# VectorE in written order, wider statistics for image 0 and a rearranged end, in a two-layer attention kernel

## The chip, the cores and the metric

The kernel runs on one core of one Trainium2 chip. The metric is the device time of one execution in microseconds (us), the median of several runs.

## The reference, cut to what matters

Two attentions follow each other on 8 images of 64 channels and 64 x 64 = 4096 positions, all in float32.

```python
# layer 0: 8-channel f and g, 64-channel values
f, g, hh = Wf @ x + bf, Wg @ x + bg, Wh @ x + bh
x = x + hh @ softmax(f^T g, axis=2)^T
# layer 1: group norm (8 groups), then 64-channel attention
xn = (x - mu) * rsqrt(var + 1e-5) * gamma + beta
q, k, v = split(w_qkv @ xn + b_qkv)
out = x + w_proj @ attention(q, k, v, scale=64**-0.5) + b_proj
```

## The kernel before

The work is laid out as a list of *stages*, one per layer and image, in the order L0 image 0, L0 image 1, L1 image 0, L0 image 2, L1 image 1 and so on. A stage has 4 chunks of 512 queries, and a chunk 16 *steps*. In each step TensorE makes scores into PSUM, ScalarE takes their exponentials into one of six `e` buffers, TensorE multiplies the `e` of the step before by the values into accumulators, and VectorE adds that `e` into a running sum, `esum` (128 x 2048 elements, 2.29 us). Everything else (projections, copies of values, statistics of the group norm, reciprocals) is a *unit of work* due at a given step, for a later stage or a former chunk.

```python
def pair():                       # PSUM: 8 banks; three pairs rotate
    if lent is not None: return pairs[lent]
    turn += 1; return pairs[turn % 3]

def values(self, src, w, c):      # values of the next image, chunk c
    ps = pair()
    ...                           # 64x64 matmuls into ps
    first_ = self.kind == self.b == c == 0
    copy = nc.vector.tensor_copy if lent is None or first_ else nc.scalar.copy
    copy(self.vt[:, :, ts(c, TPC), :], ps[...])

def weigh(i, j, e, cols, now):    # values x e, and the add into esum
    at.weigh(acc, e[:, p], t, p, j == 0, j == 2 * NT - 1, cols)
    ...
    with tc.issue_after(layers0[0].split.ins) if i == 0 and t == 1 else nullcontext():
        added = nc.vector.tensor_add(esum, first if t == 1 else esum, e).ins
    if t == NT - 1:
        finished(i, now)          # copies the accumulators away (total), later sums and result

def total(self, raw, acc):        # layer 1: VectorE empties both accumulator banks
    nc.vector.tensor_copy(raw, acc[0])
    return nc.vector.tensor_add(raw, acc[1], raw)

def ended():                      # end of a step: first the due units, then weigh
    for u in due: u[2]()
    for r in batch: weigh(*r, now)
```

Names in the views: `banks` is PSUM; `vt_l` holds values; `v_l` of 128 x 512 holds values of layer 1, but `v_l` of 128 x 1 the variance of the group norm, and `mu_l` its mean; `xn_l` is the normalised input; `raw_l` takes the accumulators; `full_l`, `high_l` and `fg_l` are a projection of layer 0, its cast and the result of splitting it; `kq_l` is what scores are made from.

In this kernel only TensorE is held to the order of the program text. VectorE's instructions are ordered by a scheduler at build time, with a few hints (`issue_after`).

## Time and profile before

| | before |
|---|---|
| median of the first 3 runs | 3088.32 us (3088.18 to 3089.82) |
| span of the profiled run | 3087.7 us |
| TensorE busy | 3050.4 us (99%) |
| VectorE busy | 2534.7 us (82%) |

Two views carry the reading. The first is the page's line of busy tenths, the span in 40 slices of 77 us: each digit is the busy share of a slice in tenths.

```profile
DVE  7998877899768997689876898779987799876676
```

VectorE (DVE) is at nine tenths in the second and third slice, that is up to 231 us. The second is the table by windows; each row is a stretch, its length, then the busy time of PE (TensorE's matmuls), PEld (its weight loads), DVE (VectorE), ACT (ScalarE) and POOL (GpSimd), with the number of instructions, and then the granted clock of TensorE, the share of the DMA engines and GB/s.

```profile
28.00:60.00 32.00, 32.00 (x249) 12.02 (x248) 30.82 (x16) 27.22 (x26) 0.00 (x0) 1.00 0.44 107
141.00:222.00 81.00, 79.25 (x470) 27.43 (x468) 78.61 (x44) 66.23 (x54) 0.00 (x0) 1.00 0.03 8
222.00:262.00 40.00, 30.22 (x148) 10.14 (x148) 35.60 (x34) 21.27 (x21) 0.00 (x0) 0.83 0.03 7
```

From 222 to 262 us, where the statistics of image 0 are made, TensorE works only 30.2 of 40 us and at a clock of 0.83; in the two stretches ahead it has hardly a gap. VectorE has hardly a gap up to 222 us.

### The profile page before, as it was taken

How to read it: one execution, taken by the hardware profiler on the slowest of the kernel's cores; microseconds unless marked ns; L12 is line 12 of the kernel's file. 1: busy time of each engine (PE TensorE's matmuls, PEld its weight loads, DVE VectorE, ACT ScalarE, POOL GpSimd, SP SyncE). 2: the span in 40 equal slices, each digit the busy share in tenths (PEclk: the TensorE clock that was granted, in tenths of full speed). 3: DMA queues.
4: the chain of work that ended last, by engine and by line, in shares of the span. 5: the costliest groups of instructions: out<-in, count | busy, mean ns of one | idle time of the engine just before them, and what ended most of it. 6: DMA issues, size and time to landing. Idle time of an engine off the chain costs nothing.

```text
span 3087.7 us, 59407 instructions
## 1 busy us (share of the span) xinstructions
PE 3050.4 (99%) x26083; PEld 1133.9 (37%) x26083; DVE 2534.7 (82%) x1612; ACT 2043.5 (66%) x1999; POOL 16.5 (1%) x45
## 2 busy tenths in 40 slices
PE   8999999999999999999999999999999999999998
PEld 3333334333343333433334333343333333333433
DVE  7998877899768997689876898779987799876676
ACT  6876655786557865578655785558855588555554
POOL 2000000000000000000000000000000000000000
PEclk9999999999999999999999999999999999999999
DMA  3000010100101001010010100100001000000000
GB/s 78 22 8 11 18 39 15 32 1 15 39 15 32 1 15 39 22 25 1 15 39 22 25 1 17 41 22 22 1 25 36 19 8 1 15 22 15 9 15 12
DMA packets 57531, 62.54 MB, mean 20 GB/s; under 512 B 30816, under 2 KB 30864, under 8 KB 57264
## 3 DMA queue, kind: packets, MB, share of 16 engines
q1 hardware_dynamic: 56192, 58.38, 7.6%
q8 instruction: 206, 3.38, 0.4%
q14 instruction: 61, 0.50, 0.1%
q0 software_dynamic: 672, 0.12, 0.0%
q10 hardware_dynamic: 400, 0.17, 0.0%
HBM read 25.06 MB, written 8.65 MB: 11 GB/s over the span
## 4 chain that ended last, share of the span: by engine, by line
PE 94%; DVE 4%; issue 1%; ACT 1%; DMA 0%; SPq 0%; DVEq 0%; ACTq 0%
PE banks L137 94%; DVE esum_l L749 3%; ACT e_l L836 0%; ACT e_l L877 0%; DVE vt_l L322 0%; DMA x<-in_x_dram 0%; DVE esum_l L386 0%; DVE esum_l L335 0%; ACT full_l L501 0%; SPq L166 0%; DVE high_l L506 0%; DVE diag L401 0%; DVE w_l L589 0%; DVE raw_l L374 0%; DVE x L540 0%
## 5 line engine op out<-in xcount | busy, mean ns | idle before, releaser
L749 DVE TENSOR_TENSOR esum_l<-esum_l,e_l 128x2048 f32<-128x2048 f32 x895 | 2050.1, 2291 | 462.0 <-ACT e_l L836 403.8
L836 ACT ACTIVATE e_l<-banks 128x1024 f32<-128x1024 f32 x1024 | 992.9, 1021 | 800.2 <-PE banks L137 776.8
L137 PE MATMUL banks<-e_l,v_l 64*64 64x512 f32 (+2 forms) x8772 | 1102.7, 589 | 0.0
L877 ACT ACTIVATE e_l<-banks 128x2048 f32<-128x2048 f32 (+3 forms) x765 | 956.2, 1314 | 195.7 <-PE banks L137 188.5
L137 PE MATMUL banks<-kq_l 64*64 64x512 f32 (+1 forms) x8448 | 1009.8, 586 | 2.5 <-ACT mu_l L567 1.2
L137 PE MATMUL banks<-e_l,vt_l 128*64 128x512 f32 (+1 forms) x4060 | 832.1, 550 | 0.0
L137 PEld LDWEIGHTS banks<-e_l,v_l 64*64 64x64 f32 (+1 forms) x8772 | 362.6, 133 | 576.1 <-issue 529.2
L137 PEld LDWEIGHTS banks<-kq_l 64*64 64x64 f32 (+1 forms) x8448 | 348.0, 135 | 577.7 <-issue 545.8
L137 PEld LDWEIGHTS banks<-e_l,vt_l 128*64 128x64 f32 x4060 | 266.9, 136 | 471.5 <-issue 451.4
L137 PE MATMUL banks<-fg_l 32*128 32x512 f32 x1792 | 209.5, 459 | 4.9 <-ACT e_l L877 3.3
L749 DVE TENSOR_TENSOR esum_l<-e_l,e_l 128x2048 f32<-128x2048 f32 x64 | 146.4, 2288 | 11.4 <-ACT e_l L836 9.4
L137 PEld LDWEIGHTS banks<-fg_l 32*128 32x128 f32 x1792 | 85.3, 182 | 187.4 <-ACT e_l L877 138.7
L335 DVE TENSOR_TENSOR esum_l<-esum_l 128x1024 f32<-128x1024 f32 x63 | 76.8, 1219 | 0.7
L654 DVE COPY raw_l<-banks 128x512 f32<-128x512 f32 x31 | 21.4, 691 | 31.3 <-PE banks L137 31.3
L628 ACT ACTIVATE kq_l<-banks,qkb 128x512 f32<-128x512 f32 x64 | 40.6, 696 | 3.8 <-PE banks L137 3.8
L374 DVE TENSOR_TENSOR raw_l<-raw_l,r_l 128x512 f32<-128x512 f32 x63 | 43.1, 684 | 0.0
L137 PE MATMUL banks<-esum_l,ones 128*32 128x256 f32 x504 | 40.3, 391 | 1.6 <-DVE vt_l L322 1.6
L137 PE MATMUL banks<-xn_l,wqk 64*64 64x512 f32 x256 | 34.3, 607 | 4.0 <-DVE xn_l L596 4.0
L137 PEld LDWEIGHTS banks<-wh,x 64*64 64x64 f32 x1024 | 23.2, 138 | 15.6 <-issue 14.4
L137 PEld LDWEIGHTS banks<-wvp,xn_l 64*64 64x64 f32 x1024 | 20.6, 134 | 16.8 <-issue 16.8
L536 ACT COPY raw_l<-banks 128x512 f32<-128x512 f32 x32 | 19.0, 595 | 11.6 <-PE banks L137 11.4
L540 DVE SCALAR_TENSOR_TENSOR x<-raw_l,hb,x 128x512 f32<-128x512 f32 x32 | 24.0, 751 | 1.1
(108 smaller groups left out, 391.7 us busy)
## 6 DMA issues: line engine op xcount, KB each, us to landing
r_l<-recips SPq DMA_DIRECT2D x126, 128.0 KB, 2.9
fg_l<-high_l SPq DMA_DIRECT2D x216, 64.0 KB, 2.0
kq_l<-kq_l SPq DMA_DIRECT2D x64, 128.0 KB, 2.3
out_dram<-raw_l SPq DMA_DIRECT2D x62, 128.0 KB, 2.4
x<-in_x_dram SPq DMA_DIRECT2D x30, 256.0 KB, 4.7
zt_l<-zs_l SPq DMA_DIRECT2D x252, 1.0 KB, 1.7
kq_l<-high_l SPq DMA_DIRECT2D x32, 64.0 KB, 2.0
recips<-stash SPq DMA_DIRECT2D x63, 4.0 KB, 1.4
```

Source lines behind the costliest of these rows:

```text
L137: in_order(nc.tensor.matmul(*args, **kwargs))
L335: nc.vector.tensor_add(esum[:, 0], esum[:, 0], esum[:, 1])
L374: nc.vector.tensor_mul(raw, raw, r)
L536: nc.scalar.copy(raw, acc[0])
L540: nc.vector.scalar_tensor_tensor(xc, o, hb, xc, op0=ALU.add, op1=ALU.add)
L628: nc.scalar.activation(self.parts[:, h, cols], ps[:, h, :], AF.Identity, bias=k1["qkb"][:, h : h + 1],)
L654: nc.vector.tensor_copy(raw, acc[0])
L749: added = nc.vector.tensor_add(esum, first if t == 1 else esum, e).ins
L836: nc.scalar.activation(e[:, p], both_ps[p], AF.Exp, scale=at.scale)
L877: nc.scalar.activation(e.rearrange("k p h n -> k (p h) n")[:, first_ : first_ + n_, :], banks[:, bank : bank + n_, :], AF.Exp, scale=at.scale,
```

## The change

Its intent is to take VectorE's order out of the scheduler's hands. Every VectorE instruction goes through a wrapper that ties it behind the one written before it. The statistics of image 0 are spaced one step wider, and the last chunk's code is put into the order in which its inputs come. The core of the diff:

```diff
+    class InOrder:
+        def __getattr__(self, name):
+            def made(*args, **kwargs):
+                in_order(getattr(nc.vector, name)(*args, **kwargs), "vector")
+            return made
+    vector = InOrder()
 ...                                  # then nc.vector.* -> vector.* everywhere, hints removed, e.g.
-            with tc.issue_after(layers0[0].split.ins) if i == 0 and t == 1 else nullcontext():
-                added = nc.vector.tensor_add(esum, first if t == 1 else esum, e).ins
+            vector.tensor_add(esum, first if t == 1 else esum, e)
 ...                                  # Layer1.before(): statistics, all images and image 0
-            at = [18, 21, 24] if self.b == 0 else [16, 20, 24]
+            at = [18, 22, 26] if self.b == 0 else [16, 20, 24]
-                s = 30 + 8 * c
+                s = 31 + 8 * c if self.b == 0 else 30 + 8 * c
-                    (s - 3, lambda c=c: normal(c), False),
+                    (s - 4, lambda c=c: normal(c), False),
 ...                                  # end(): the accumulators ahead of the reciprocal
+            self.total(raw, acc)
-            nc.vector.reciprocal(rt, z)
-            bounds(rt, 1)
+            vector.reciprocal(rt, z)
 ...                                  # each half's broadcast matmul right behind its diag;
 ...                                  # bounds and n_bad behind both
-            self.residual(raw, c, (nc.sync, nc.scalar))
+            self.residual(raw, c)     # both stores started by one engine
```

More of the change, by code (lines that the diff above doesn't have):

```diff
@@ L1 @@
-from contextlib import ExitStack, nullcontext
+from contextlib import ExitStack
 import concourse.bass as bass
@@ L120, in pair, with in_order @@
         return pairs[turn % 3]
-    tensor_last = None
-    def in_order(made):
-        nonlocal tensor_last
-        if tensor_last is not None:
+    made_last = {}
+    def in_order(made, engine="tensor"):
+        if engine in made_last:
             tc.add_manual_dep(
                 made.ins,
-                tensor_last.name,
+                made_last[engine].name,
                 mybir.DependencyInfo(mybir.DependencyClass.NoSync, mybir.DependencyReason.DATA),
@@ L133, in in_order @@
             )
-        tensor_last = made.ins
+        made_last[engine] = made.ins
+    class InOrder:
[4 more added lines that the diff above has]
+    vector = InOrder()
     def matmul(*args, **kwargs):
@@ L320, in values @@
             first_ = self.kind == self.b == c == 0
-            copy = nc.vector.tensor_copy if lent is None or first_ else nc.scalar.copy
+            copy = vector.tensor_copy if lent is None or first_ else nc.scalar.copy
             copy(
@@ L330, in finish @@
             raw = work.tile([P, CW], F32, tag="raw", bufs=4, name=f"raw_{n}")
-            copied = self.total(raw, acc)
+            self.total(raw, acc)
             zt = small.tile([P, QP], F32, tag="zt", bufs=4, name=f"zt_{n}")
             width = CW // 2
-            with tc.issue_after(copied.ins if self.kind == 1 else added):
-                nc.vector.tensor_add(esum[:, 0], esum[:, 0], esum[:, 1])
+            vector.tensor_add(esum[:, 0], esum[:, 0], esum[:, 1])
             r = None
@@ L364, in reciprocals @@
                 rt = stash[:, ts(index, QP)]
-                nc.vector.reciprocal(rt, zt)
+                vector.reciprocal(rt, zt)
                 broadcast()
@@ L373, in result @@
             def result():
-                nc.vector.tensor_mul(raw, raw, r)
+                vector.tensor_mul(raw, raw, r)
                 self.residual(raw, c)
@@ L383, in end @@
             total = esum[:, 0]
-            with tc.issue_after(added):
-                for part in (esum[:, 1], e[:, 0], e[:, 1]):
-                    nc.vector.tensor_add(total, total, part)
+            for part in (esum[:, 1], e[:, 0], e[:, 1]):
+                vector.tensor_add(total, total, part)
             z, laid = pair()[:, 0, 0:QP], pair()[:, 0, :]
@@ L394, in end @@
                 )
+            raw = work.tile([P, CW], F32, tag="raw", bufs=4, name="raw_end")
+            self.total(raw, acc)
             rt = small.tile([P, QP], F32, tag="zt", bufs=4, name="rt")
-            nc.vector.reciprocal(rt, z)
-            bounds(rt, 1)
-            raw = work.tile([P, CW], F32, tag="raw", bufs=4, name="raw_end")
+            vector.reciprocal(rt, z)
             diag = work.tile([P, QP, P], F32, tag="full", bufs=1, name="diag")
             for h in range(2):
-                nc.vector.tensor_mul(
+                vector.tensor_mul(
                     diag[:, ts(h, TPC), :],
@@ L405, in end @@
                 )
-            self.total(raw, acc)
-            for i in range(2):
-                matmul(bad_ps, bad[:, i : i + 1], ones[:, 0:1], start=i == 0, stop=i == 1)
-            nc.vector.tensor_copy(n_bad, bad_ps)
-            for h in range(2):
                 matmul(
@@ L414, in end @@
                 )
-            nc.vector.tensor_mul(raw, raw, laid)
-            self.residual(raw, c, (nc.sync, nc.scalar))
+            bounds(rt, 1)
+            for i in range(2):
+                matmul(bad_ps, bad[:, i : i + 1], ones[:, 0:1], start=i == 0, stop=i == 1)
+            vector.tensor_copy(n_bad, bad_ps)
+            vector.tensor_mul(raw, raw, laid)
+            self.residual(raw, c)
     class Layer0(Attention):
@@ L481, in project_direct @@
                 )
-                nc.vector.tensor_copy(high[:, i, :], full[:, i, :])
-                nc.vector.scalar_tensor_tensor(
+                vector.tensor_copy(high[:, i, :], full[:, i, :])
+                vector.scalar_tensor_tensor(
                     dst[:, 0:CW], high[:, i, :].bitcast(F32), lowmask2[:, i : i + 1],
@@ L502, in project @@
             high = work.tile([P, 2, CW], F32R, tag="high", bufs=1, name=f"high_{n}")
-            nc.vector.tensor_copy(high[rows], full[rows])
+            vector.tensor_copy(high[rows], full[rows])
             split = high
-            self.split = nc.vector.scalar_tensor_tensor(
+            vector.scalar_tensor_tensor(
                 split[rows], high[rows].bitcast(F32), lowmask[rows, :], full[rows],
@@ L539, in residual @@
             xc = x_tiles[self.b][:, ts(c, CW)]
-            nc.vector.scalar_tensor_tensor(xc, o, hb, xc, op0=ALU.add, op1=ALU.add)
-            nc.vector.bn_stats(self.st[:, c, :], xc)
+            vector.scalar_tensor_tensor(xc, o, hb, xc, op0=ALU.add, op1=ALU.add)
+            vector.bn_stats(self.st[:, c, :], xc)
     class Layer1(Attention):
@@ L560, in channels @@
             def channels():
-                nc.vector.bn_aggr(mv, self.st())
+                vector.bn_aggr(mv, self.st())
             def means():
@@ L568, in means @@
                 d = small.tile([P, 1], F32, tag="d", name=f"d_{n}")
-                nc.vector.tensor_sub(d, mv[:, 0:1], mu)
-                nc.vector.scalar_tensor_tensor(v, d, d, mv[:, 1:2], op0=ALU.mult, op1=ALU.add)
+                vector.tensor_sub(d, mv[:, 0:1], mu)
+                vector.scalar_tensor_tensor(v, d, d, mv[:, 1:2], op0=ALU.mult, op1=ALU.add)
             def deviations():
@@ L576, in deviations @@
                 nc.scalar.copy(ve, ps[:, 0, 0:1])
-                nc.vector.tensor_scalar_add(ve, ve, EPS)
+                vector.tensor_scalar_add(ve, ve, EPS)
                 guess = small.tile([P, 1], I32, tag="guess", name=f"guess_{n}")
-                nc.vector.tensor_single_scalar(
+                vector.tensor_single_scalar(
                     guess, ve.bitcast(I32), 1, op=ALU.logical_shift_right
                 )
-                nc.vector.tensor_scalar(
+                vector.tensor_scalar(
                     guess, guess, -1.0, float(0x5F3759DF), op0=ALU.mult, op1=ALU.add
@@ L588, in deviations @@
                 for i in range(4):
-                    nc.vector.scalar_tensor_tensor(w, y, y, ve, op0=ALU.mult, op1=ALU.mult)
-                    nc.vector.tensor_scalar(w, w, -0.5, 1.5, op0=ALU.mult, op1=ALU.add)
-                    nc.vector.tensor_mul(y, y, w)
-                nc.vector.tensor_mul(self.a, y, k1["gam"])
+                    vector.scalar_tensor_tensor(w, y, y, ve, op0=ALU.mult, op1=ALU.mult)
+                    vector.tensor_scalar(w, w, -0.5, 1.5, op0=ALU.mult, op1=ALU.add)
+                    vector.tensor_mul(y, y, w)
+                vector.tensor_mul(self.a, y, k1["gam"])
             def normal(c):
                 xns[c] = work.tile([P, CW], F32, tag="xn", bufs=1, name=f"xn_{n}_{c}")
-                nc.vector.tensor_scalar(
+                vector.tensor_scalar(
                     xns[c], x_tiles[self.b][:, ts(c, CW)], mu, self.a,
@@ L653, in total, with residual @@
         def total(self, raw, acc):
-            nc.vector.tensor_copy(raw, acc[0])
-            return nc.vector.tensor_add(raw, acc[1], raw)
-        def residual(self, o, c, queues=(nc.sync, nc.sync)):
-            nc.vector.scalar_tensor_tensor(
+            vector.tensor_copy(raw, acc[0])
+            vector.tensor_add(raw, acc[1], raw)
+        def residual(self, o, c):
+            vector.scalar_tensor_tensor(
                 o, o, k1["pb"], x_tiles[self.b][:, ts(c, CW)], op0=ALU.add, op1=ALU.add
@@ L661, in residual @@
             for h in range(2):
-                queues[h].dma_start(out[self.b, :, ds(h * NH + c * CW, CW)], o[ts(h, C), :])
+                nc.sync.dma_start(out[self.b, :, ds(h * NH + c * CW, CW)], o[ts(h, C), :])
             if c == NC - 1 and self.b + 3 < B:
@@ L712, in fast_path @@
     acc = esum = first = None
-    added = None
     def due_part(ready, room):
@@ L734, in weigh @@
     def weigh(i, j, e, cols, now):
-        nonlocal acc, esum, first, added
+        nonlocal acc, esum, first
         at, c = seq[i]
@@ L778, in finished @@
             steps = (now + delay + wait, now + delay + 2 * wait)
-        def behind(work_):
-            def made():
-                with tc.issue_after(added):
-                    work_()
-            return made
-        at_step(steps[0], behind(reciprocals), 0)
-        at_step(steps[1], behind(result), 0)
+        at_step(steps[0], reciprocals, 0)
+        at_step(steps[1], result, 0)
     closed = 1
@@ L810, in bounds @@
         ok = work.tile(list(recip.shape), F32, tag="raw", bufs=4, name=f"ok_{i}")
-        nc.vector.tensor_scalar(ok, recip, 1.0 / SUM_MAX, None, op0=ALU.is_ge)
-        nc.vector.scalar_tensor_tensor(
+        vector.tensor_scalar(ok, recip, 1.0 / SUM_MAX, None, op0=ALU.is_ge)
+        vector.scalar_tensor_tensor(
             ok, recip, 1.0 / SUM_MIN, ok, op0=ALU.is_le, op1=ALU.mult
@@ L815, in bounds @@
         least = small.tile([P, 1], F32, tag="least", name=f"least_{i}")
-        nc.vector.tensor_reduce(least, ok, axis=AX.X, op=ALU.min)
-        nc.vector.tensor_scalar(bad[:, i : i + 1], least, -1.0, 1.0, op0=ALU.mult, op1=ALU.add)
+        vector.tensor_reduce(least, ok, axis=AX.X, op=ALU.min)
+        vector.tensor_scalar(bad[:, i : i + 1], least, -1.0, 1.0, op0=ALU.mult, op1=ALU.add)
     at_step(len(seq) * NT - 3, lambda: bounds(stash, 0), 0)
```

## The prediction

> **What bounds the kernel now.** I read the page first. Its busy line and its chain of work name TensorE:
>
> ```profile
> PE 3050.4 (99%) x26083; PEld 1133.9 (37%) x26083; DVE 2534.7 (82%) x1612; ACT 2043.5 (66%) x1999; POOL 16.5 (1%) x45
> ...
> PE 94%; DVE 4%; issue 1%; ACT 1%; DMA 0%; SPq 0%; DVEq 0%; ACTq 0%
> ```
>
> Of 3087.7 us only 37.3 are without a matmul. A change that touches no matmul can win those, plus time in which TensorE ran at half clock or stood in a weight load. So I asked who makes TensorE wait (all waits, longest first; columns: engine, what it waited for, us in total, times, longest):
>
> ```profile
> PEld banks L137 <- DVE vt_l L322: 6.9, 6, 1.2
> ...
> PE banks L137 <- DVE v_l L570: 4.5, 1, 4.5
> PE banks L137 <- DVE xn_l L596: 4.0, 1, 4.0
> ```
>
> Two single waits of 4.5 and 4.0 us belong to the statistics of image 0; six waits of 1.2 us recur once per image. The merged chain in order of time shows that VectorE carries it without a gap from 141.6 to 256.6 us, and that TensorE has 219 us to itself after that. The timeline of this stretch has the two waits:
>
> ```profile
> 234.71 0.15 DVE L569 TENSOR_TENSOR d_l<-mv_l,mu_l 128x1 f32<-128x1 f32 x1
> 234.90 0.22 DVE L570 SCALAR_TENSOR_TENSOR v_l<-d_l,mv_l 128x1 f32<-128x1 f32 x1
> 235.18 0.50 PEld L137 LDWEIGHTS banks<-v_l,gavg 128*128 128x128 f32 x2 [4.82 <-DVE v_l L570]
> ...
> 256.58 0.30 PEld L137 LDWEIGHTS banks<-xn_l,wqk 64*64 64x64 f32 x8 [4.40 <-DVE xn_l L596]
> ```
>
> mu was copied by ScalarE at 226.23, but four adds of 2.29 us (225.3 to 234.7) stood on VectorE ahead of the two small operations. The same happens to the Newton steps: adds are strewn among them from 242.7 to 255.6.
>
> The table by windows gives granted clock 0.57 in 234 to 242 us and 0.55 in 256 to 263, where 248 to 254 has 1.00: after each wait some 6 us at half speed, so about 3 us lost each time.
>
> **VectorE is the hidden bound of the first 260 us.** It is busy 30.82 of 32, 38.82 of 40 and 39.65 of 41 us in the windows from 28 to 141. An add starts every 2.385 us, while TensorE needs 35.6 us for 16 steps of layer 0 (2.22 each; chunk of 177.7 to 213.3). ScalarE waits for VectorE four times (4.9 us in all) around 219 to 225: the six e buffers are full. This caps the gain: TensorE can't run more than six steps ahead of the adds.
>
> **What the Trainium skill says.** "TensorE: Matmul & The Clock Gate", Part 1, says that a TensorE idle for about 3.4 us drops to half clock until it has been busy as long; the trace agrees (0.57, 0.55). The same page (engine queue depths) says that ScalarE and VectorE take their queue strictly first in, first out: so the order in the program is the order on the engine, and one waiting instruction holds all behind it. The trace agrees: d_l, ready from 226.4, ran at 234.71. "DMA: Bandwidth & Descriptors", section "Issuing engines are not separate DMA queues", says that starting DMAs on several engines saves only the sequencer's time; here one store takes it 0.47 to 0.57 us.
>
> **The change part by part.**
>
> No arithmetic is added or taken away. Written order means: in each step the due pieces of work (copies of values, reciprocals, statistics) come first, then the add for the step before, and at a chunk's end the copy of the accumulators.
>
> (1) *Start.* Now the copy of the values (13.59) is in front of the second split (14.20), which had its input at 12.25. Written order puts the split first, so the chain split, full_l (15.06), and all behind it moves by about 14.20 - 12.29 = **1.9 us** earlier.
>
> (2) *Statistics of image 0.* With d and v after about two adds in place of five, and the second matmul four steps after the first in place of three, the 4.5 us wait goes. The 17 operations on [128,1] (3.3 us in one block, as at 435.85 to 439.15 for image 1) and xn come after add 88 in place of 94: xn is ready at about 246 in place of 256.5, as five or six adds of 2.385 us move behind it. TensorE comes to xn then, paced by VectorE, and waits little. Recovered: 4.5 + 4.0 + 1.8 (waits for mu and mv) + 2 x 3 of cold clock = 16 us at most. Against this VectorE, saturated, loses 1 to 5 us where written order makes it wait for ScalarE's full_l at two projections of image 1 (full ready at 49.5 and 89.6, now taken at 54.3 and 95.4). It has about 13 us idle between 258.7 and 348 to repay with. I take **10 us**.
>
> (3) *Values copied by VectorE in layer 1.* Six times the copy is behind an add:
>
> ```profile
> 478.09 2.29 DVE L749 TENSOR_TENSOR esum_l<-esum_l,e_l 128x2048 f32<-128x2048 f32 x1 [1.13 <-ACT e_l L836]
> ...
> 480.30 0.68 DVE L322 COPY vt_l<-banks 128x512 f32<-128x512 f32 x1
> 481.03 0.16 PEld L137 LDWEIGHTS banks<-esum_l,ones 128*32 128x32 f32 x8 [1.16 <-DVE vt_l L322]
> ```
>
> Weight loads come every 0.43 us, so the one after 479.65 was due at 480.08: 0.95 us lost. In written order the copy runs at 477.3, in the idle time before the add. 6 x 0.95 = **5.7 us** won.
>
> (4) *The same at a chunk's boundary: a loss.* At steps 32 and 48 of each layer-1 stage that prepares another image (7 stages, by the 28 VectorE copies of v_l at four each), values are due in the very step in which a chunk ends:
>
> ```profile
> 520.52 2.29 DVE L749 TENSOR_TENSOR esum_l<-esum_l,e_l 128x2048 f32<-128x2048 f32 x1 [2.01 <-ACT e_l L836]
> ...
> 523.25 0.69 DVE L322 COPY v_l<-banks 128x512 f32<-128x512 f32 x1 [0.43 <-PE banks L137]
> ...
> 524.93 0.69 DVE L654 COPY raw_l<-banks 128x512 f32<-128x512 f32 x1 [0.54 <-PE banks L137]
> 525.73 0.69 DVE L655 TENSOR_TENSOR raw_l<-banks,raw_l 128x512 f32<-128x512 f32 x1
> 526.01 0.14 PEld L137 LDWEIGHTS banks<-e_l,v_l 64*64 64x64 f32 x2 [0.28 <-issue]
> ...
> 526.44 0.23 PEld L137 LDWEIGHTS banks<-e_l,v_l 64*64 64x64 f32 x6 [0.29 <-issue]
> ```
>
> The second accumulator comes free at 526.42, and TensorE's first matmul of the next chunk is at 526.44: no slack at all. In written order the copy of v, which can't start before 523.25, comes ahead of the add. From there: copy 0.61 to the next start, add 2.21, accumulator copy 0.80, second 0.69: free at 527.56. TensorE stands for 527.58 - 526.44 = 1.14 us. 14 x 1.14 = **16 us** lost. The other boundaries (start of a stage, step 16) have no copy in front; all other work due in a layer-1 step meets 1.14 us of idle VectorE per step of 3.43 us and is caught up before anyone needs it.
>
> (5) *End.* The accumulators move into the time in which TensorE makes the sums (73.7 to 75.7 after 3000), and the broadcast's first half starts at about 76.65 in place of 78.28. At half clock it still needs about 2.8 us for both halves, and the check (its matmul and n_bad) now stands before the last product: product at about 79.9 in place of 80.30. Two stores through one queue cost 0.55 us more for the second. Sum about **0**.
>
> Sum: 3088.3 - 1.9 - 10 - 5.7 + 16 + 0 = 3086.7 us. As (4) is the one part that can only be smaller, I say **3085 us**.
>
> **Rivals.** (a) *The boundary costs nothing*, as a copy might still be issued after the add: then 3071. Against it: each VectorE instruction is now tied to the one written before. One chance in six. (b) *VectorE stays the bound of the first 340 us*, so that the statistics only move the wait: part 2 brings 2 to 4 in place of 10, and the time is about 3092. For it speaks 96% busy from 28 to 141 us. Against it: the 13 us of idle later. One in five. (c) *Written order blocks VectorE on a DMA* (reciprocals back from memory): the result now starts 7.2 us after its reciprocal, without a wait; written four steps apart they get more than that. Unlikely; some 5 us. (d) *All is hidden*: TensorE at 99% goes on as it did. The waits were TensorE's own, so their going must show.
>
> **Range and chances.** 80%: 3071 to 3092, from (a) with its gains to (b). Two per cent are 62 us, more than all idle time of TensorE together, and no loss that I find comes near it: within 2% at 0.98, 0.01 on either side.
>
> **What will show it.** Part 1: the first scores at about 13.5 in place of 14.99. Part 2: the waits for v_l and xn_l gone or under 1 us, granted clock 1.00 from 220 to 270 us, the first layer-1 scores about 12 us earlier than 344.15. Part 3: no wait of a weight load for vt_l. Part 4: a new wait for raw_l (the second accumulator read), 14 times about 1.1 us, once per boundary at steps 32 and 48, and the v_l copy ahead of the add there; if it is missing, I misread the order and the time is near 3070. Part 5: the span from the last add to the end within 0.6 us of before. The prediction falls if VectorE waits at a place that I took for harmless, above all for ScalarE in the saturated first stretch.

## The result and the profile after

| | before | after |
|---|---|---|
| median, 4 runs each of the same rounds | 3088.25 us (3087.93 to 3089.82) | 3096.18 us (3094.81 to 3096.63) |
| span of the profiled run | 3087.7 us | 3094.9 us |

The ratio is 1.0024 (95% interval 1.0007 to 1.0041). Such a ratio is the mean time of one kernel's runs over the mean time of the other's of the same rounds, so it isn't quite the ratio of the medians. The kernel became about 8 us slower, and the predicted range (3071 to 3092) doesn't hold 3096.

The busy times hardly differ (TensorE 3061.3 us, VectorE 2534.0). In the page's line of the chain that ended last, VectorE's share rose from 4% to 6%:

```profile
PE 92%; DVE 6%; issue 1%; ACT 1%; DMA 0%; SPq 0%; DVEq 0%; ACTq 0%
```

To see where the time went I paired the score matmuls of the two traces by their number and took the difference of their start times (after minus before). This gives a running account:

| at (us of before) | after minus before | what lies between |
|---|---|---|
| 27.6 | +2.3 | the start |
| 221 | +6.6 | the first 200 us of layer 0 |
| 224 | +7.5 | |
| 344 (first layer-1 scores, 344.15 against 337.18) | -7.0 | statistics of image 0 |
| each later image, five times | +2.0 | period 378.97 against 380.98 us |
| the fourth and the last of these seven | +2.4 | 381.33 us in the fourth; the last lacks the gain of part 3, which is there six times |
| from the last add to the end | -0.7 | 20.25 against 19.58 us |

So three losses stand against one gain. **The start.** The first scores of the kernel before waited for the split last:

```profile
14.99 0.19 PEld L137 LDWEIGHTS banks<-fg_l 32*128 32x128 f32 x4 [1.59 <-DVE fg_l L483]
```

VectorE's part of the timeline of the kernel after (start, duration, engine, line, operation, output<-input, sizes, count; in brackets the idle time before it and what ended it):

```profile
12.24 0.75 DVE L138 SCALAR_TENSOR_TENSOR fg_l<-high_direct,lowmask,full_direct 128x512 fp32r<-128x512 f32 x1
...
14.28 0.69 DVE L138 CAST high_l<-full_l 64x1024 fp32r<-64x1024 f32 x1 [1.28 <-ACT full_l L506]
15.07 1.28 DVE L138 SCALAR_TENSOR_TENSOR high_l<-high_l,fgb_low,full_l 64x1024 fp32r<-64x1024 f32 x1
16.39 0.69 DVE L138 COPY vt_l<-banks 128x512 f32<-128x512 f32 x1
17.13 0.29 PEld L145 LDWEIGHTS banks<-fg_l 32*128 32x128 f32 x4 [3.88 <-DVE vt_l L138]
```

The second split (12.24) is 1.96 us earlier than before, as predicted. But the first scores wait for the copy of the first values, which now stands behind the cast and the split of the next projection: that copy frees the PSUM pair into which the scores go. Before, the copy ran first, at 13.59, and the scores began at 14.99.

**The first 200 us.** Two of the same windows, of the kernel after:

```profile
28.00:60.00 32.00, 31.20 (x245) 11.48 (x241) 24.09 (x12) 27.34 (x26) 0.00 (x0) 1.00 0.44 112
222.00:262.00 40.00, 37.59 (x247) 13.70 (x245) 38.54 (x38) 29.79 (x30) 0.00 (x0) 1.00 0.03 7
```

In the first stretch VectorE is busy 24.1 us in place of 30.8. The largest single gap is one instruction that waits at the head of its queue, while `e` buffers that it could have added lie ready behind it:

```profile
51.84 0.69 DVE L138 CAST high_l<-full_l 128x1024 fp32r<-128x1024 f32 x1 [6.61 <-ACT full_l L506]
```

The second of them is the gain: TensorE has 37.6 of 40 us where it had 30.2, and its clock is 1.00 in place of 0.83 (0.96 in the profiles of e1 and e7, which have the same code here).

**The boundary between chunks in layer 1**, twice per image that prepares another one. The line of the waits view (engine, what it waited for, total us, times, longest), and then the timeline of one such boundary:

```profile
PEld banks L145 <- DVE raw_l L138: 24.6, 28, 1.1
```

```profile
458.55 0.68 DVE L138 COPY raw_l<-banks 128x512 f32<-128x512 f32 x1
459.29 0.19 PEld L145 LDWEIGHTS banks<-e_l,v_l 64*64 64x64 f32 x4 [1.13 <-DVE raw_l L138]
...
459.34 0.69 DVE L138 TENSOR_TENSOR raw_l<-banks,raw_l 128x512 f32<-128x512 f32 x1
...
460.08 0.26 PEld L145 LDWEIGHTS banks<-e_l,v_l 64*64 64x64 f32 x8 [0.60 <-DVE raw_l L138]
```

The weight loads for the next chunk wait for both accumulator reads, which are late because the copy of `v` and the add of 2.29 us were ahead of them. There are 28 such waits at 14 boundaries. The waits for the variance `v` and for `xn` of image 0 and the six for `vt` of the kernel before are gone from the list; the one wait for `vt` left (3.9 us) is the start.

### The profile page after: what moved, and what is told of

It reads as the page before. It is cut to its first block, busy times and chain, and to the rows that moved or that the text cites. A ratio compares the mean times of both kernels' runs of the same rounds, so it can differ in the third digit from the quotient of the medians.

```text
span 3094.9 us, 59415 instructions
## 1 busy us (share of the span) xinstructions
PE 3061.3 (99%) x26083; PEld 1134.4 (37%) x26083; DVE 2534.0 (82%) x1612; ACT 2044.1 (66%) x2001; POOL 17.2 (1%) x45
## 4 chain that ended last, share of the span: by engine, by line
PE 92%; DVE 6%; issue 1%; ACT 1%; DMA 0%; SPq 0%; DVEq 0%; ACTq 0%
PE banks L145 92%; DVE esum_l L138 5%; ACT e_l L873 1%; DVE raw_l L138 0%; DVE v_l L138 0%; DMA x<-in_x_dram 0%; DVE high_l L138 0%; DMA r_l<-recips 0%; DVE x L138 0%; ACT full_l L506 0%; DVE st_l L138 0%; ACT e_l L832 0%; DVE w_l L138 0%; DMA recips<-stash 0%; SPq L174 0%
## 5 line engine op out<-in xcount | busy, mean ns | idle before, releaser
L145 PE MATMUL banks<-e_l,v_l 64*64 64x512 f32 (+2 forms) x8772 | 1127.8, 588 | 3.5 <-DVE raw_l L138 3.5
L873 ACT ACTIVATE e_l<-banks 128x512 f32<-128x512 f32 (+3 forms) x767 | 956.9, 1311 | 197.4 <-PE banks L145 182.8
L145 PE MATMUL banks<-kq_l 64*64 64x512 f32 (+1 forms) x8448 | 1038.0, 586 | 3.3 <-ACT e_l L873 3.0
L145 PEld LDWEIGHTS banks<-kq_l 64*64 64x64 f32 (+1 forms) x8448 | 356.6, 134 | 577.8 <-issue 532.6
L138 DVE COPY v_l<-banks 128x512 f32<-128x512 f32 x28 | 19.4, 692 | 122.6 <-PE banks L145 122.6
L138 DVE COPY vt_l<-banks 128x512 f32<-128x512 f32 x25 | 17.3, 691 | 42.9 <-PE banks L145 42.8
L138 DVE CAST high_l<-full_l 128x1024 fp32r<-128x1024 f32 (+1 forms) x16 | 11.1, 693 | 23.7 <-ACT full_l L506 16.8
## 6 DMA issues: line engine op xcount, KB each, us to landing
x<-in_x_dram SPq DMA_DIRECT2D x30, 256.0 KB, 4.7
```

Source lines behind the costliest of these rows:

```text
L138: in_order(getattr(nc.vector, name)(*args, **kwargs), "vector")
L145: in_order(nc.tensor.matmul(*args, **kwargs))
L873: nc.scalar.activation(e.rearrange("k p h n -> k (p h) n")[:, first_ : first_ + n_, :], banks[:, bank : bank + n_, :], AF.Exp, scale=at.scale,
```

## The experiments

Theory: three places in which written order puts an instruction ahead of one that TensorE needs sooner (the start, the first 200 us, the boundary) cost what the account shows, and their costs add; the statistics gain by the order. The rivals say that a wait only shows what another limit takes anyway. All outputs were correct. The kernel before ran beside each group: 3088.45, 3089.09 and 3088.38 us in the three groups, and 3088.25 beside the kernel after. As these differ by up to 0.8 us, I compare by the difference from before; for the kernel after it is +7.9 us.

| run | edit | median us | minus before | ratio to before (95%) |
|---|---|---|---|---|
| e1 | boundary copy behind | 3079.37 | -9.1 | 0.9971 (0.9957 to 0.9984) |
| e2 | first copy on ScalarE | 3093.05 | +4.6 | 1.0014 (1.0001 to 1.0028) |
| e3 | split of image 1 later | 3091.70 | +3.2 | 1.0010 (0.9996 to 1.0023) |
| e4 | old spacing, written order | 3096.64 | +7.6 | 1.0025 (1.0011 to 1.0039) |
| e5 | before + spacing | 3089.83 | +0.7 | 1.0004 (0.9990 to 1.0018) |
| e6 | before + boundary order | 3108.76 | +19.7 | 1.0064 (1.0050 to 1.0078) |
| e7 | two queues at the end | 3096.24 | +7.9 | 1.0025 (1.0009 to 1.0040) |
| e9 | boundary copy between | 3079.85 | -9.2 | 0.9970 (0.9956 to 0.9983) |
| e10 | values behind an add | 3096.48 | +8.1 | 1.0026 (1.0012 to 1.0039) |
| e11 | before + statistics order | 3076.30 | -12.1 | 0.9961 (0.9947 to 0.9975) |
| e8 | e1, e2, e3 and e7 together | 3073.83 | -14.6 | 0.9954 (0.9941 to 0.9968) |

### e1: the boundary undone

From the kernel after:

```diff
-            copy(self.vt[...], ps[...])
+            made = lambda: copy(self.vt[...], ps[...])
+            if put_off is None: made()
+            else: put_off.append(made)
 ...                               # ended(), at the last step of a layer-1 chunk
+        put_off = [] if bound and seq[batch[-1][0]][0].kind == 1 else None
         for u in due: u[2]()
         for r in batch: weigh(*r, now)
+        for made in put_off or []: made()
```

> The changed kernel with one thing undone: at the chunk boundaries of layer 1 the copy of the values is written behind the last add and the two accumulator copies, where the scheduler had it before. Theory (the copy ahead of the add costs a wait for the second accumulator, 14 boundaries, 1.11 to 1.18 us each): 14 x 1.15 = 16 us less than the changed kernel, about 3080 us; no weight load waits for the second accumulator read (raw) any more; period of one image 378.7 us in place of 380.98. Rival (the wait only shows what another limit would take anyway, such as ScalarE or the exps): the waits go, the time stays within 4 us of 3096.

Measured: 17.0 us less than the kernel after (-9.1 against +7.9), the period of an image 378.66 us in place of 380.98, no wait for `raw` by a weight load left. The boundary in its timeline:

```profile
457.13 0.69 DVE L139 COPY raw_l<-banks 128x512 f32<-128x512 f32 x1 [2.06 <-PE banks L146]
...
459.67 0.68 DVE L139 COPY v_l<-banks 128x512 f32<-128x512 f32 x1
460.40 0.21 PEld L146 LDWEIGHTS banks<-kq_l 64*64 64x64 f32 x8 [0.68 <-DVE v_l L139]
```

VectorE now waits for the accumulators (2.06 us) and not TensorE for VectorE. Per boundary this is (380.98 - 378.66) / 2 = 1.16 us, 16.2 us for 14 of them. The theory holds and the rival falls. In the profiled run a further 0.9 us lies in the end, where TensorE happened to keep its full clock (below, under e7).

### e9: does the new wait for the copy cost anything?

The last line above shows 0.68 us of waiting for the copy that e1 moved. e9 puts that copy between the add and the accumulator copies, the scheduler's own order:

```diff
             vector.tensor_add(esum, first if t == 1 else esum, e)
+        for made in put_off or []: made()
+        put_off = None
         if t == NT - 1:
             finished(i, now)
```

> The changed kernel with the boundary's copy of values between the last add and the accumulator copies, the scheduler's order to the letter. It is compared with the run that puts it behind the accumulator copies, where the weight load after it shows 14 waits of 0.68 us for this copy. Theory (that wait only coincides with the half of the weight loads that the second accumulator set back by 0.43 us, so the order between doesn't matter as long as the add is ahead): within 1.5 us of that run, about 3079 us, period 378.6 to 378.8 us. Rival (the waits are real): 14 x 0.38 to 0.48 us = 5 to 7 us less, about 3073 us, period 377.9.

Measured: 0.2 us less than e1 by the differences from before, period 378.61 to 378.63 us (one image 378.95) against 378.66. The theory holds: the 14 waits of 0.68 us are gone from the list, and they were worth (378.66 - 378.62) / 2 = 0.02 us each. A line of waits is not a line of costs.

### e6: the boundary's order alone, in the kernel before

```diff
-            copy(
+            copied_v = copy(
                 self.vt[...], ps[...])
 ...
+            if at.kind == 1 and t == NT - 1 and copied_v is not None:
+                behind_ = copied_v           # the last add is tied behind the copy
```

> The kernel before with one thing of the change alone: at the layer-1 chunk boundaries where values are copied, the last add is tied behind that copy; all else as the scheduler has it. Theory: the loss of the boundary comes from this order alone, 14 x 1.1 to 1.2 = 16 us: about 3104.5 us, waits of a weight load for raw 14 or 28 times, up to 1.1 us each. Rival (the loss needs other parts of the written order too): within 4 us of the kernel before.

Measured: +19.7 us, period 381.84 in place of 378.97, so 1.44 us per boundary: the order alone makes the loss, and more of it than I expected. Its timeline shows the difference:

```profile
465.32 0.68 DVE L656 COPY raw_l<-banks 128x512 f32<-128x512 f32 x1
465.92 0.54 DVE L598 TENSOR_SCALAR xn_l<-x,mu_l,a_l 128x512 f32<-128x512 f32 x1
466.06 0.19 PEld L138 LDWEIGHTS banks<-e_l,v_l 64*64 64x64 f32 x4 [1.13 <-DVE raw_l L656]
...
466.37 0.68 DVE L657 TENSOR_TENSOR raw_l<-banks,raw_l 128x512 f32<-128x512 f32 x1
...
467.11 0.21 PEld L138 LDWEIGHTS banks<-e_l,v_l 64*64 64x64 f32 x8 [0.86 <-DVE raw_l L657]
```

The scheduler, left free otherwise, put the next normalisation between the two accumulator reads, and the second wait grew from 0.60 to 0.86 us. The miss in size, 0.28 us per boundary, fits the 0.26 us by which this second wait grew; the first wait, 1.13 us, is the same as in the kernel after.

### e2: the start

```diff
-            copy = vector.tensor_copy if lent is None or first_ else nc.scalar.copy
+            copy = vector.tensor_copy if lent is None and not first_ else nc.scalar.copy
```

> The changed kernel with the first copy of values taken by ScalarE, so that VectorE doesn't put it behind the split. Theory (the first scores wait for the bank pair that this copy frees, not for the split alone): first scores at 14.0 to 15.0 us in place of 17.1, and the lead of 2 to 3 us is kept to the end: 3093 to 3094 us. Rival 1 (VectorE is the bound of the first 220 us, so an earlier start only fills the e buffers earlier): start 2 to 3 us earlier but under 1 us left by step 88, 3095 to 3096. Rival 2: ScalarE's own queue delays the first exps by the copy, first scores no earlier than 16.

```profile
13.77 0.58 ACT L330 COPY vt_l<-banks 128x512 f32<-128x512 f32 x1 [1.98 <-PE banks L145]
...
14.40 0.19 PEld L145 LDWEIGHTS banks<-fg_l 32*128 32x128 f32 x4 [0.82 <-ACT vt_l L330]
```

Measured (the line of the copy is ScalarE's): first scores at 14.40 in place of 17.13, and 3.3 us less in the median. The split was ready at 13.03 (12.28 and 0.75 long) and the scores still waited for the copy: it is the copy's PSUM pair that they need. In the profiled run, of the lead of 2.8 us that stood at 179 us, 1.85 us were left behind the statistics of image 0, where VectorE sets the pace, and 2.2 us at the last scores. By this run rival 1 would be right for about a third of the lead. But it was the slowest of the five (3094.66, 1.6 us above the median), and the 3.3 us of the median are more than the whole lead, so the share of rival 1 stays open.

### e3: the first 200 us

In image 1's two projections the cast, the split and their DMAs become a unit of their own, due three steps later:

```diff
-            vector.tensor_copy(high[rows], full[rows])
-            ...                              # split and DMAs
+            def cut():
+                vector.tensor_copy(high[rows], full[rows])
+                ...                          # split and DMAs
 ...
+            cuts = [(s + 3, lambda: self.cut(), False) for s in at] if self.b == 1 else []
```

> The changed kernel with the cast and split of image 1's two projections written three steps after their matmuls. Theory (VectorE, saturated from 28 to 222 us, loses what it waits there for ScalarE's projection output, 6.6 us at 51.8 alone, and TensorE gets it later as full e buffers): that wait gone or under 1 us, VectorE over 29 of 32 us busy in 28 to 60, score matmuls at 222 us some 3 to 5 us earlier than in the changed kernel, 3091 to 3093 us. Rival (the loss is repaid in VectorE's idle time after 258 us, or TensorE is the bound there): under 1 us of it arrives at the end, 3095 to 3096.

```profile
51.91 0.68 DVE L138 CAST high_l<-full_l 128x1024 fp32r<-128x1024 f32 x1
```

Measured: `full_l` was ready at 51.38, and the cast follows an add without a wait; VectorE is busy 30.25 of the 32 us from 28 to 60, the score matmuls are 4.5 us earlier at 204 us, and all of it arrives (4.7 us in the median). This was inside what the theory expected, and the rival, that VectorE's later idle time repays the loss, falls.

### e4 and e5: the spacing of the statistics

e4 is the kernel after with the three numbers of the spacing set back; e5 is the kernel before with them set forward.

```diff
-            at = [18, 22, 26] if self.b == 0 else [16, 20, 24]     # e4; e5 is the reverse
+            at = [18, 21, 24] if self.b == 0 else [16, 20, 24]
```

> The changed kernel with the old spacing of image 0's statistics. Theory (VectorE runs some five steps behind TensorE there, so one step less between two statistics lets TensorE wait about one step of 2.2 to 2.4 us more, and half clock follows a wait of 4 us): TensorE waits 2 to 4 us for v or mv and again for xn, first layer-1 scores 3 to 8 us later than in the changed kernel (337.18), time 3099 to 3104. Rival (the order alone wins it): within 1 us of the changed kernel, 3095 to 3097.

> The kernel before with the wider spacing of image 0's statistics alone, VectorE still ordered by the scheduler. Theory (the 14 us are won by the order, as adds stand among the Newton steps in the scheduler's order): the wait for v goes (4.5 us and some 2 us of half clock), the wait for xn of 3 to 4 us stays; first layer-1 scores at 338 to 342 us in place of 344.15, time 3082 to 3087. Rival (the spacing does it all): both waits gone, first layer-1 scores near 334, time about 3078 to 3079, 10 us under the kernel before.

Measured: e4 is within 0.4 us of the kernel after, and its layer-1 scores at 342 us come 0.2 us earlier than there. e5 is within 0.8 us of the kernel before. **Both of my theories fell here**: the wider spacing is worth nothing, with written order or without. In e4 the rival, order alone, is right. In e5 neither was: the wait for `v` went, and the wait for `xn` grew to three times its length, so that the first layer-1 scores came 0.2 us later than before.

```profile
233.68 9.47 DVE L749 TENSOR_TENSOR esum_l<-esum_l,e_l 128x2048 f32<-128x2048 f32 x4
...
257.03 0.54 DVE L596 TENSOR_SCALAR xn_l<-x,mu_l,a_l 128x512 f32<-128x512 f32 x1
257.62 0.30 PEld L137 LDWEIGHTS banks<-xn_l,wqk 64*64 64x64 f32 x8 [13.19 <-DVE xn_l L596]
```

From 233.68 to 257.03 VectorE makes nine adds and 16 small operations, and `xn` comes behind them all. TensorE, 13 us ahead, can't move until then. A new theory follows: in this stretch VectorE is the bound, so what counts is only which of its work stands ahead of `xn`.

### e11: the statistics' order alone, in the kernel before

Old spacing, scheduler's order, and one tie: the adds of the second layer-0 stage go behind the statistics of image 0 that are written ahead of them.

```diff
-                nc.vector.bn_aggr(mv, self.st())
+                noted(nc.vector.bn_aggr(mv, self.st()), self.b)   # also v, a and xn
 ...
+            if at.kind == 0 and at.b == 1 and stat_last is not None:
+                behind_ = stat_last
```

> The kernel before, old spacing, scheduler's order, with one thing of the change alone: the adds of the second layer-0 stage are tied behind the statistics of image 0 (and its normalised values) that are written ahead of them. Theory (the gain of the statistics comes from their place ahead of the adds, and from nothing else): waits for v and xn gone or under 1 us, first layer-1 scores about 13 to 15 us earlier than 344.15, period of an image 378.97 as before, time 3073 to 3076. Rival 1 (order and spacing are needed together): under 6 us of gain. Rival 2 (VectorE stays the bound and the wait moves on, as with the spacing alone): first layer-1 scores within 2 us of 344.

Measured: -12.1 us; the score matmuls lead the kernel before by 0.6 us at 202 us and by 13.2 us from 262 us to the end, with the period unchanged (378.97). The waits for `v` and `xn` are gone.

```profile
226.95 0.15 DVE L575 TENSOR_TENSOR d_l<-mv_l,mu_l 128x1 f32<-128x1 f32 x1
...
239.52 0.54 DVE L602 TENSOR_SCALAR xn_l<-x,mu_l,a_l 128x512 f32<-128x512 f32 x1
239.97 16.60 DVE L758 TENSOR_TENSOR esum_l<-esum_l,e_l 128x2048 f32<-128x2048 f32 x7
...
246.01 0.21 PEld L143 LDWEIGHTS banks<-xn_l,wqk 64*64 64x64 f32 x8 [0.37 <-issue]
```

`mu` is taken up 1.15 us after its copy (225.80 to 226.95), where it waited 8.3 us before (226.38 to 234.71). `xn` is made at 239.5 in place of 256.0, with seven adds behind it, and TensorE comes to it at 246.0 without a wait. The new theory holds: the place ahead of the adds alone brings 12.6 us, where the written order moved the account by 14.4 us in this stretch. Where the other 1.8 us come from isn't shown.

### e10: the values ahead of the sums

From the kernel after, the second copy of the next image's values is written behind the add of its step:

```diff
-            if put_off is None:
+            if put_off is None or self.kind == 1 or c != 1:
                 made()
```

> The changed kernel with the second copy of the next image's values in layer 1 (the one just ahead of the sums' matmul) written behind the add of its step, as the scheduler had it. Theory (a switch to the sums' weights takes 0.81 us in any case, so only what the wait of 1.16 us has above that counts): period of an image up by 0.25 to 0.35 us to 381.3, 6 times, 2 us in all: 3097 to 3099. Rival (the prediction's reading, 0.95 us each): period up by 0.95 us, 6 us in all: 3101 to 3103.

```profile
472.58 0.69 DVE L139 COPY vt_l<-banks 128x512 f32<-128x512 f32 x1
...
475.08 0.16 PEld L146 LDWEIGHTS banks<-esum_l,ones 128*32 128x32 f32 x8 [0.81 <-issue]
```

Measured: no change (+0.2 us, period 380.98). Both expectations missed: even behind the adds the copy ended at 473.27, 1.8 us before the sums' weight load, so the edit didn't bring the wait back. The run doesn't size the effect. It does show that this weight load takes 0.81 us of idle time with nothing to wait for; e9 sizes it (below).

### e7: two queues at the end

```diff
-            self.residual(raw, c)
+            self.residual(raw, c, (nc.sync, nc.scalar))
```

> The changed kernel with its last two stores started by two engines, as before. Theory (one queue starts them one after the other, 0.96 us each, so the second starts a store's time later): time from the last add to the end 0.5 to 1.0 us less than the 19.58 us of the changed kernel, total 3095 to 3096. Rival (the second store's start is hidden behind the first store's transfer): within 0.2 us of 19.58.

The stores in the kernel after, and in e7:

```profile
3088.96 1.92 SPq L667 DMA_DIRECT2D out_dram<-raw_end  x2
```

```profile
3089.11 0.47 SPq L667 DMA_DIRECT2D out_dram<-raw_end  x1
3089.11 0.52 ACTq L667 DMA_DIRECT2D out_dram<-raw_end  x1
```

Measured: 19.21 us from the last add to the end in place of 19.58, so 0.4 us, between the two expectations, and nothing in the median. (e8, also with two queues, took 19.16 us.) The clock matters more there: in e1 the broadcast matmuls ran at full clock (1.68 us in place of 2.57), and its end took 18.65 us with one queue. In e9, with the same code at the end as e1, they took 2.57 us again, so the order of the code doesn't set which of the two a run gets.

### e8: the version that beats both

e1, e2, e3 and e7 in one kernel.

> The three edits together (values copy behind at boundaries, first copy on ScalarE, split of image 1 three steps later), with the last two stores on two queues. Theory (the losses are at different places and add): 3096 - 16 - 2.5 - 4 - 0.5 = about 3073 us, 3071 to 3077, faster than both kernels. Rival (the start and the first stretch share one bound, so their gains don't add): 3077 to 3080.

Measured: 3073.83 us, 14.6 us under the kernel before and 22.6 under the kernel after; the interval of the ratio (0.9941 to 0.9968) excludes 1. The four edits alone sum to 17.0 + 3.3 + 4.7 + 0.1 = 25.1 us, so 2.5 us don't add. In the spans of the profiled runs it is 24.6 us against 22.9, and most of this difference lies in which runs were profiled: one image of the kernel after took 381.33 us in place of 380.98 (also in e4, e7 and e10, but not in e1, e2, e3 and e8), which each of the three differences counts (0.7 us too much), and e1's end kept the full clock (0.9 us), which e8's did not. Behind the statistics e2 and e3 lead by 1.85 and 4.55 us, and e8, which has no boundary up to there, by 6.0, so at least 0.4 us overlap. It may be more, for e8 had luck at its start: the first projection matmuls took 0.65 us where e2's took 1.12, and its first scores came at 12.79 in place of 14.40. In the main the losses were at different places, as the theory says; how much the start and the first stretch share isn't settled. e11, one tie in the kernel before, has 12.1 of the 14.6 us: it takes the gain and leaves the scheduler's good order at the start and the boundary alone.

## Why the prediction was wrong, point by point

Its account, and what the runs showed:

| part | predicted | measured | by |
|---|---|---|---|
| 1 start | -1.9 us | +2.3 | traces, e2 |
| 2 statistics and first stretch | -10 | -9.3 | traces, e3, e11 |
| 3 values ahead of the sums | -5.7 | -2.1 | traces, e9 |
| 4 boundary | +16 | +16.2 | e1, e6 |
| 5 end | 0 | -0.7 | traces, e7 |
| sum | -1.6 | +6.4 | spans: +7.2 |

**Part 1 failed in sign.** The step that failed is "the chain split, full_l (15.06), and all behind it moves by about 1.9 us earlier". The split and `full_l` did move (12.24 and 13.13), but the scores depend on the copy of the values as well, through the PSUM pair that it empties. I followed the data from split to scores and didn't ask which other instruction has to free their output. That is 4.2 us between prediction and account. The size depends on the clock of the profiled run. In the order of the kernel before, the first scores came at 14.99 and 14.96 (before, e6) where the first projection matmuls took 1.12 us, and at 13.62 (e5) where they took 0.65; in written order they came at 17.07 to 17.15 in all seven profiles that have its start, with 0.65 as with 1.12. So the loss was between 2.1 and 3.5 us.

**Part 2 was right in its sum and half right in its reasons.** From 224 to 344 us the account moves by 14.4 us (predicted: 16 at most), and up to there the first stretch loses 5.2 us, which the prediction had named only as "1 to 5 us" (6.6 us of waiting in one place). e3 shows that this loss is real and never repaid, against my "about 13 us idle between 258.7 and 348 to repay with". The step that failed is "the second matmul four steps after the first in place of three, the 4.5 us wait goes": e4 and e5 show the spacing to be worth nothing. The order of adds and small operations, which the prediction also named, brings 12.6 us by itself (e11). That 9.3 us came so near to 10 is partly luck: the prediction took 6 us off its 16 for a loss that it expected to be in part repaid, and the whole loss stayed. (Its "17 operations" are 16 in the trace of image 1.) The rival (b), VectorE as the bound, was true of this stretch in so far as TensorE came to `xn` behind VectorE's adds (e5), but its forecast, 2 to 4 us in place of 10, was not.

**Part 3 was right in mechanism and mis-sized.** The wait of 1.16 us went, six times. The term that failed is "so the one after 479.65 was due at 480.08". This load would have come 0.94 us after its predecessor in any case, as 26 of the 32 switches from the 64-row weights of layer 1's scores to the 128-row weights of the sums do in the kernel before, and all 32 in the kernel after; the six with the wait came after 1.29. So 0.35 us each were to be had, and 6 x 0.35 = 2.1 us. The periods agree: e9 has before's order at the boundary and lacks the wait, 378.97 - 378.62 = 0.35 us per image.

**Part 4 held.** Predicted 1.14 us, 14 times; measured 1.16. The copy of `v` ahead of the add, the waits for both accumulators and their count are as foretold.

**Part 5** moved by 0.7 us the other way, of which the single queue took back 0.4. It is of the size of the clock's phase there (0.9 us) and I can't divide it further.

**The range.** Correcting parts 1 and 3 in the prediction's own sum gives 3086.7 + 4.2 + 3.6 = 3094.5 us, within 2 us of what was measured. The other fault was to shave 1.7 us off that sum with the argument that part 4 could only be smaller, and to set the upper end (3092) by one rival only, while the start and the first stretch could each lose a few us as well. The closing sentence of the prediction, that it falls "if VectorE waits at a place that I took for harmless, above all for ScalarE in the saturated first stretch", names one of the causes.

What stays open: 0.8 us between the sum of the parts and the spans, and a further 0.7 us between spans and medians. Of the 0.8 us, 0.35 are the long image (381.33 us), and 0.3 come if the boundary is read against e9 (1.18 us in place of 1.16, 14 times). The rest is below what the start alone differs by from run to run.

## What to carry to other kernels

When an in-order engine serves a saturated one, go through its queue asking of each instruction who waits for it next and whether its own input is there: a copy that frees a PSUM bank is as urgent as the data, and an instruction whose input comes late must not stand ahead of work that is ready. Fixing the whole order by the program text gives control, but it takes over the text's bad places with the good ones; here one tie (e11) had most of the gain, and the full order paid only once the boundary was rewritten (e1, 9.1 us under the kernel before), and most with three places rewritten (e8, 14.6 us). And a wait in a profile costs only what it adds to the same transition where nobody waits: 1.16 us was worth 0.35 us, and 0.68 us was worth 0.02 us.

## What the Trainium skill lacked or had wrong

- "TensorE: Matmul & The Clock Gate", Part 1, gives some 3.4 us, as the least, both for losing the full clock and for winning it back. For losing it, less was enough here: in the kernel before the clock fell at 234.95 after 4.3 us without a matmul, but at 255.43 after 2.8 us, and in e1, e2, e4, e7, e10 and e11 it fell between 227 and 231 us with no gap over 1.5 us in the 8 us ahead. In the kernel after, e3, e8 and e9 a gap of the same length left it at 1.00. The half clock then lasted 3.4 us in these six. Elsewhere winning it back took more than the least: in the kernel before from 235.2 and from 256.6 it took 6.6 and 5.7 us to 1.00, and in e5 from 257.6 about 5.2 us. So where the prediction says that the trace agrees, it does so for the half clock and not for these times. An estimate of what a wait costs should use these.
- No page has a number for a switch between tile sizes ("TensorEngine Tiling (Array Packing)", Key Properties, says only that a change of tiling mode drains TensorE; "TensorE: Matmul & The Clock Gate", Part 3, that a weight load overlaps matmuls in flight only where the row groups differ). Here a change from the 64-row weights of the scores to the 128-row weights of the sums comes 0.94 us after the load before it, against 0.41 us at a change between weights of equal shape, also where nothing is waited for (e10: 0.81 us idle, "issue"). That the rows are the reason is my reading; no run here tests it, and other changes of the row count in the kernel before took other times (the 32-row scores of layer 0 to the sums mostly 0.55 us).
- "DMA: Bandwidth & Descriptors", on issuing engines, says that starting DMAs from several engines saves only sequencer time. The runs agree and give the number: the two last stores took one sequencer 1.92 us and two sequencers 0.47 and 0.52 us in parallel, which moved the end by 0.4 us (e7).
